# A conv and state-space network on one core: layer 0's parameters turned as one tile, and the first images loaded earlier

## The chip, the cores and the metric

The kernel runs on one core of a Trainium2 chip. The metric is the device time of one execution in microseconds (us), as the median of several runs. Five engines work side by side, each with its own instruction queue: PE (TensorE, matrix products; PEld is its loading of weights), DVE (VectorE), ACT (ScalarE), POOL (GpSimd) and SP (SyncE, which here does nothing but issue transfers). An engine takes its instructions in the order in which they stand in its queue; an instruction that must wait for another engine or a transfer holds up all that stands behind it.

## What is computed

Layer 0 is an inverted-residual block on 32 images of 96 channels and 56 x 56 pixels, layer 1 a block of two selective state-space (Mamba) steps over the 3136 pixels of each image. What matters here is layer 0:

```python
h = conv1x1(x, fake_quant(w1))            # 96 -> 576 channels
h = silu(bn(h, g1, b1, m1, v1))
h = depthwise3x3(h, fake_quant(w2))       # each channel by itself, 9 taps
h = silu(bn(h, g2, b2, m2, v2))
s = silu(mean(h) @ se_w1.T + se_b1)       # 24 values per image
s = sigmoid(s @ se_w2.T + se_b2)          # a gate per channel
h = conv1x1(h * s, fake_quant(w3))        # 576 -> 96
x = x + bn(h, g3, b3, m3, v3)
...
x = layer1(x)
```

`fake_quant` rounds a weight tensor to 255 steps of its largest absolute value; `bn` is a scale `inv` and a shift `sh` per channel.

## The kernel before

Layer 0 keeps the 576 hidden channels in five tiles of up to 128 partitions (`NCT` = 5; the last, `FOLD`, has 64 channels and holds the upper half of the image on 64 partitions and the lower half on the other 64). For each image, `expand` (line 212) makes a hidden tile with matmuls of `w1` and writes it with ACT (line 225) into one of three padded buffers `hpad`. The nine taps of a tile are then done in one of two ways: tiles 2 and 3 with nine passes of DVE (`taps_dve`, lines 300 and 302; `FOLD` likewise, 314 and 316), tiles 0 and 1 (`PE_TILES`) with 32 x 32 matmuls on PE (`taps_pe`, line 276), with ACT's silu behind them (line 283). The silu needs the scale and shift of the second normalisation per partition.

On PE the taps write each group of 32 channels to a place that depends on the band of rows: in band `r` of four, group `gr` goes to group `(gr + r) % 4`. So what stands on a partition in band `r` is another channel than in band 0, and every per-channel parameter used afterwards is needed in four turned copies. `SEEN` lists the eleven versions (two tiles in four bands, and the three others as they are); `NSEE` = 11. The turned parameters are the scale `tinv`, the shift `tsh`, the gate's bias `tseb`, the last convolution's weights `tw3` (96 columns) and the first gate weights `tsew1` (24 columns). They are made by `turned` (line 149), which for each of the five copies each version with transfers inside SBUF: one for an unturned tile, two for `FOLD`, four for a turned one. All are issued by SP (line 161), as are the loads of the weights (line 110) and of the images (line 210, `load_x`). `folded` (line 164) does the like for three small parameters of `FOLD`.

The order of the start: the scheduler of the language places the instructions of everything ahead of `tc.manual_schedule()`; inside it, the order is the one written. SP's queue holds the weight loads, then the turning and folding, then the first three images, and then per image four stores of `x1d` and one load. DVE's queue holds two of the three clearings of `hpad` (line 200), the maxima for the quantisation (line 130), the normalisations (lines 85 to 88), 44 small copies (line 184), the third clearing, the quantisation (lines 132 to 138), the diagonal tap weights (line 193), the clearing of `hfold` (line 203), and then the taps of image 0.

Of the kernel before, what the change touches and what calls it, by code (L numbers as in the profile page):

```python
# [11 lines left out]
F32 = mybir.dt.float32  # L12
# [7 lines left out]
B, C, H, W = 32, 96, 56, 56  # L20
L = H * W
HID, RED = 576, 24
NCT = 5
# [17 lines left out]
FOLD = NCT - 1  # L41

SEEN = [(ct, r) for ct in PE_TILES for r in range(4)] + [(ct, 0) for ct in range(NCT) if ct not in PE_TILES]
NSEE = len(SEEN)


G1, B1, M1, V1, G2, B2, M2, V2, SEB2, TAP = 0, 1, 2, 3, 4, 5, 6, 7, 8, 9
# [6 lines left out]
def conv_mamba_kernel(ctx, tc, a, out):  # L54
    nc = tc.nc
    v, s, g, pe, sp = nc.vector, nc.scalar, nc.gpsimd, nc.tensor, nc.sync
# [23 lines left out]
    def bn_fold(pool, gam, bet, mean, var, p, n, name):  # L80

        inv = pool.tile([p, n], F32, name=f"inv{name}", tag=f"inv{name}")
        sh = pool.tile([p, n], F32, name=f"sh{name}", tag=f"sh{name}")
        s.activation(inv, var, AF.Sqrt, bias=epsc[:p])
        v.reciprocal(inv, inv)
        v.tensor_mul(inv, inv, gam)
        v.tensor_mul(sh, mean, inv)
        v.tensor_sub(sh, bet, sh)
        return inv, sh
# [5 lines left out]
    with ExitStack() as ph:  # L95
        wts = ph.enter_context(tc.tile_pool(name="l0w", bufs=1))
        small = ph.enter_context(tc.tile_pool(name="l0s", bufs=2))
        xin = ph.enter_context(tc.tile_pool(name="l0x", bufs=3))
# [9 lines left out]
        def loadw(name, shape):  # L108
            t = wts.tile(list(shape), F32, name=name, tag=name)
            sp.dma_start(t, a[name])  # L110
            return t

        def wtile(name, shape):
            return wts.tile(list(shape), F32, name=name, tag=name)

        hp = loadw("hp", [128, NCT, NHP])
        w1 = loadw("w1", [C, HID])
        w3 = loadw("w3", [128, NCT, C])
        sew1 = loadw("sew1", [128, NCT, RED])
        sew2 = loadw("sew2", [RED, NCT, 128])  # L120
        seb1 = loadw("seb1", [RED, 1])

        def fake_quant(w, p, shape, name):

            mx = small.tile([p, 1], F32, name=f"mx{name}", tag=f"mx{name}", bufs=1)
            sc = small.tile([p, 1], F32, name=f"sc{name}", tag=f"sc{name}", bufs=1)
            rs = small.tile([p, 1], F32, name=f"rs{name}", tag=f"rs{name}", bufs=1)
            q = small.tile([p, *shape], F32, name=f"q{name}", tag=f"q{name}", bufs=1)
            axis = AX.X if len(shape) == 1 else AX.XY
            v.tensor_reduce(mx, w, axis, ALU.max, apply_absolute_value=True)  # L130
            g.partition_all_reduce(sc, mx, p, bass_isa.ReduceOp.max)
            v.tensor_scalar(sc, sc, 1.0 / 127.0, None, ALU.mult)
            v.reciprocal(rs, sc)
            v.tensor_scalar(q, w, rs, None, ALU.mult)
            v.tensor_scalar(q, q, ROUND, ROUND, ALU.add, ALU.subtract)
            v.tensor_scalar(q, q, sc, None, ALU.mult)
            v.tensor_sub(q, q, w)
            v.tensor_add(w, w, q)

        fake_quant(w1, C, [HID], "w1")  # L140
        fake_quant(hp[:, :, TAP : TAP + 9], 128, [NCT, 9], "w2")
        fake_quant(w3, 128, [NCT, C], "w3")
# [2 lines left out]
        inv2, sh2 = bn_fold(wts, hp[:, :, G2], hp[:, :, B2], hp[:, :, M2], hp[:, :, V2], 128, NCT, "2")  # L145
        inv3, sh3 = bn_fold(wts, cp[:, G3 : G3 + 1], cp[:, B3 : B3 + 1], cp[:, M3 : M3 + 1], cp[:, V3 : V3 + 1], C, 1, "3")


        def turned(name, t, shape):
            to = wtile(name, [128, NSEE, *shape])  # L150
            for e, (ct, r) in enumerate(SEEN):
                if ct == FOLD:
                    parts = [(slice(h * 64, h * 64 + 64), slice(0, 64)) for h in range(2)]
                elif r == 0:
                    parts = [(slice(0, 128), slice(0, 128))]
                else:
                    parts = [
                        (slice(q * 32, q * 32 + 32), slice((q - r) % 4 * 32, (q - r) % 4 * 32 + 32)) for q in range(4)
                    ]
                for rows, src in parts:  # L160
                    sp.dma_start(to[rows, e], t[src, ct])
            return to

        def folded(name, t):

# [6 lines left out]
        fsh = folded("fsh", sh1[:, FOLD : FOLD + 1])  # L172
        ftap = folded("ftap", hp[:, FOLD, TAP : TAP + 9])

        tinv = turned("tinv", inv2.unsqueeze(2), [1])
        tsh = turned("tsh", sh2.unsqueeze(2), [1])
        tseb = turned("tseb", hp[:, :, SEB2 : SEB2 + 1], [1])
        tw3 = turned("tw3", w3, [C])
        tsew1 = turned("tsew1", sew1, [RED])
        tsew2 = wtile("tsew2", [RED, NSEE, 128])  # L180
        for e, (ct, r) in enumerate(SEEN):
            for q in range(4):
                src = q % 2 * 32 if ct == FOLD else (q - r) % 4 * 32
# [14 lines left out]
        for i in range(NHB):  # L198
            t = hp3.tile([128, H + 2, W + 2], F32, name=f"hpad{i}", tag=f"hpad{i}")
# [1 line left out]
            hpad.append(t)  # L201
        hfold = hp3.tile([128, H // 2 + 2, W + 2], F32, name="hfold", tag="hfold")
        v.memset(hfold, 0.0)

        xs, maps, h2s, pools, se = {}, {}, {}, {}, {}

        def load_x(b):
            if b < B:
                xs[b] = xin.tile([C, L], F32, name=f"x{b}", tag="x")
                sp.dma_start(xs[b], a["x"][b])  # L210

        def expand(b, ct, qs):
            if not 0 <= b < B:
# [187 lines left out]

        P0, P1 = PE_TILES
        D0, D1 = (ct for ct in range(NCT) if ct not in PE_TILES and ct != FOLD)
        load_x(0)
        load_x(1)
        with tc.manual_schedule():
            expand(0, D0, range(4))
            expand(0, P0, range(4))
            for b in range(B + 1):
# [18 lines left out]
                silu_dve(b, D0, 1)  # L428
                project(b - 1, 1)
                load_x(b + 2)  # L430
                expand(b, P1, range(4))
                taps_dve(b, D1, 0, range(6, 9))
# [15 lines left out]
    with ExitStack() as ph:  # L448
# [65 lines left out]
        for i in range(NL):  # L514
# [8 lines left out]
            for h in range(2):  # L523
                cols = slice(h * C, h * C + C)
                ps = bank(f"cw_{i}_{h}")
                for o in range(KC + 1):
                    to = ps[: C + 1, o * C : o * C + C]
# [17 lines left out]
        for h in range(2):  # L545
            for i in range(NL):
                to = wd[h * 64 + 2 * NS : h * 64 + 2 * NS + RANK, i, :, :]
# [6 lines left out]
        for i in range(NL):  # L554
            for k in range(NB):
                for h in range(2):
                    r = slice(h * 64, h * 64 + 64)
                    v.tensor_scalar(dd[r, i, k, :], eye[r, r], dp[r, i, k, 1:2], None, ALU.mult)

        for k in range(NB):  # L560
            ps = bank(f"wf_{k}")
            for h in range(2):
                r = slice(h * 64, h * 64 + 64)
# [464 lines left out]
```

## Time and profile before

| what | value |
|---|---|
| median of 3 runs | 19243.92 us (19236.5 to 19254.51) |
| the profiled execution: its time | 19246.5 us |
| the profiled execution: its span | 19243.6 us |
| layer 0, with the start | about the first 3300 us |
| DVE busy, share of the span | 18041.5 us, 94% |
| DVE busy in the first 50 us | 24.8 us |
| POOL / PE / ACT busy, share of the span | 81% / 75% / 74% |
| one pass of a tap on DVE (line 302), mean | 1989 ns, 1024 times |
| issue of one turning transfer on SP, median | 589 ns, 150 times |

Times in a profile are counted from the start of the span. In a line of the timeline, the first number is the start, the second the length in us of the whole group, then come the engine ("SPq" is SP's issuing of transfers), the line of the kernel, the operation, what it writes and reads, how often, and in brackets how long the engine had been idle and what ended that. A line of waits names who waited for whom: total us, number of times, and the longest.

### The profile page before, as it was taken

To read this page: it belongs to the slowest core of one execution; us is meant where nothing else is said; L and a number is where in the kernel's file an instruction comes from. 1 tells how busy PE (TensorE), PEld (TensorE's weight loads), DVE (VectorE), ACT (ScalarE), POOL (GpSimd) and SP (SyncE) were. 2 spreads that over 40 slices of the span, in tenths; PEclk is the share of its full clock that TensorE was granted. 3 is DMA by queue.
4 is the path that set the end of the run, shared out by engine and by line. 5 is a ranking of instruction groups with operands and counts; after the bars stand their busy time and mean duration, and the time that the engine had idled before them with its cause. 6 is when DMAs were issued, how large, how long until landed. Compare 5 with 4: busy or idle time off the path is not lost.

```text
span 19243.6 us, 282933 instructions
## 1 busy us (share of the span) xinstructions
PE 14489.7 (75%) x105692; PEld 5827.2 (30%) x105692; DVE 18041.5 (94%) x13684; ACT 14174.9 (74%) x23979; POOL 15509.9 (81%) x6606
## 2 busy tenths in 40 slices
PE   7999999677777777777777777777777777777760
PEld 3544444222222222222222222222222222222220
DVE  7888888699999999999999999999999999999993
ACT  3444444688888888888888888888888888888872
POOL 0000000699999999999999999999999999999991
PEclk9999999787777777877787778777877777778875
DMA  1000000355555555555555555555555555555548
GB/s 27 23 26 27 22 26 22 117 163 164 161 161 164 162 161 162 163 163 164 163 163 161 164 163 161 161 163 163 161 161 163 163 164 162 163 162 164 162 159 246
DMA packets 1049037, 2679.90 MB, mean 139 GB/s; under 512 B 129592, under 2 KB 342928, under 8 KB 1035368
## 3 DMA queue, kind: packets, MB, share of 16 engines
q1 hardware_dynamic: 1047656, 2661.80, 43.9%
q8 instruction: 828, 13.57, 0.3%
q14 instruction: 553, 4.53, 0.1%
HBM read 2211.05 MB, written 449.58 MB: 138 GB/s over the span
## 4 chain that ended last, share of the span: by engine, by line
DVE 35%; issue 24%; ACT 22%; PE 12%; POOL 4%; DMA 2%; SPq 1%; DVEq 0%; POOLq 0%; ACTq 0%
DVE hh L863 18%; DVE hc L871 12%; ACT da L831 5%; ACT L587 4%; ACT L588 3%; PE dw L276 3%; PE c L374 3%; POOL bx L851 2%; ACT cp L839 2%; DVE h L302 2%; DMA lr<-x1d 2%; PE bc L700 1%; PE c L223 1%; ACT dl L587 1%; ACT z L587 1%
## 5 line engine op out<-in xcount | busy, mean ns | idle before, releaser
L851 POOL TENSOR_TENSOR bx<-ub,B 128x1568 f32<-128x1568 f32 x3072 | 10975.8, 3573 | 25.2 <-DMA ub<-ud 15.8
L863 DVE TENSOR_TENSOR_SCAN hh<-da,state,bx 128x784 f32<-128x784 f32 x4608 | 8307.1, 1835 | 50.4 <-ACT da L831 44.8
L831 ACT ACTIVATE da<-deltab,acol 128x784 f32<-128x784 f32 x6144 | 5631.3, 917 | 2158.3 <-DVE hh L863 2124.2
L878 POOL TENSOR_TENSOR hc<-hh,C 128x544 f32<-128x544 f32 x3072 | 4210.3, 1371 | 40.2 <-DVE hh L863 28.8
L675 PE MATMUL xs<-xn,wx 97*64 97x392 f32 x12288 | 2907.0, 610 | 1356.5 <-DVE xn L663 1355.9
L871 DVE TENSOR_TENSOR hc<-hh,cp 128x1024 f32<-128x1024 f32 x3072 | 3667.7, 1194 | 0.1
L903 PE MATMUL y<-hc,rel 128*32 128x392 f32 x24576 | 3016.7, 579 | 367.7 <-DVE hc L871 349.2
L377 POOL TENSOR_TENSOR x<-x,x 96x784 f32<-96x784 f32 x128 | 276.5, 2160 | 3148.6 <-ACT x L376 3110.6
L863 DVE TENSOR_TENSOR_SCAN hh<-da,bx 128x784 f32<-128x784 f32 x1536 | 2679.1, 1774 | 53.4 <-ACT da L831 52.6
L675 PEld LDWEIGHTS xs<-xn,wx 97*64 97x64 f32 x12288 | 1307.8, 165 | 2982.0 <-DVE xn L663 1675.1
L302 DVE SCALAR_TENSOR_TENSOR h<-hpad,hp,h 128x1568 f32<-128x1568 f32 x1024 | 2036.3, 1989 | 34.3
L839 ACT COPY cp<-C 128x512 f32<-128x512 f32 x3072 | 1793.7, 584 | 371.6 <-DVE hc L871 369.2
L700 PE MATMUL bc<-xc,wbc 64*64 64x392 f32 x3072 | 975.5, 798 | 655.9 <-ACT xc L587 655.9
L903 PEld LDWEIGHTS y<-hc,rel 128*32 128x32 f32 x24576 | 579.8, 116 | 2092.5 <-issue 1155.1
L276 PE MATMUL dw<-hpad,diag 32*32 32x392 f32 x36864 | 1101.7, 515 | 38.6 <-issue 38.1
L691 PE MATMUL z<-xn,wz 97*64 97x392 f32 x3072 | 729.4, 555 | 480.4 <-ACT xc L686 462.3
L587 ACT ACT_TABLE_LOAD x768 | 985.3, 1283 | 13.8
L374 PE MATMUL c<-h,w3s 128*96 128x392 f32 (+1 forms) x2560 | 963.6, 521 | 40.3 <-DVE w3s L359 40.3
L588 ACT ACT_TABLE_LOAD x768 | 985.3, 1283 | 11.4
L223 PE MATMUL c<-x,w 96*128 96x392 f32 x2048 | 807.9, 551 | 193.1 <-DMA x<-in_x_dram 112.7
L283 ACT ACTIVATE h<-dw,tsh,tinv 128x392 f32<-128x392 f32 x512 | 340.0, 674 | 728.8 <-PE dw L276 728.8
L773 PE MATMUL o<-z,outw 64*96 64x392 f32 x3072 | 796.4, 652 | 97.4 <-DVE z L914 96.7
(156 smaller groups left out, 15639.9 us busy)
## 6 DMA issues: line engine op xcount, KB each, us to landing
deltab<-deltad SPq DMA_DIRECT2D x1536, 392.0 KB, 5.4
ub<-ud SPq DMA_DIRECT2D x1536, 392.0 KB, 5.8
B<-bcd SPq DMA_DIRECT2D x1024, 392.0 KB, 4.3
C<-bcd SPq DMA_DIRECT2D x1024, 392.0 KB, 4.2
deltad<-dl SPq DMA_DIRECT2D x512, 294.0 KB, 3.6
ud<-us SPq DMA_DIRECT2D x512, 294.0 KB, 3.6
x<-in_x_dram SPq DMA_DIRECT2D x32, 1176.0 KB, 7.4
x1d<-x SPq DMA_DIRECT2D x128, 294.0 KB, 2.6
```

Source lines behind the costliest of these rows:

```text
L276: pe.matmul(ps[r][to : to + 32, :HB], diag[src, n, t, :], hb[src, r0 : r0 + RB, dx : dx + W], start=t == 0, stop=t == 8, skip_group_check= ...
L302: v.scalar_tensor_tensor(acc, src, tap, acc, ALU.mult, ALU.add)
L587: s.activation(t, t, func)
L588: s.preload_act_table_set(MAIN)
L675: pe.matmul(d["xs", k][h * 64 : h * 64 + 64, :HB], wx[:, i, o, k * 64 : k * 64 + 64], xn[:, o + h * HB : o + h * HB + HB], start=o == 0, s ...
L831: s.activation(das[at][:, :LC], d["delta", k][:, p, :], AF.Exp, scale=acol[:, j, i, 2 * k + p : 2 * k + p + 1])
L839: s.copy(cps[at], data[n]["C", j][:, :LP])
L851: g.tensor_mul(bx, data[n]["u", k], beside(data[n]["B", j]))
L863: v.tensor_tensor_scan(hhs[at - p][:, p, :], das.pop(at)[:, :LC], bxs.pop(at), state[i][:, t : t + 1] if c % NQ else 0.0, ALU.mult, ALU.add,)
L871: v.tensor_mul(hcs[at - 1][:, :, :LP], hhs[at - 1][:, :, :LP], beside(cps.pop(at)))
L878: g.tensor_mul(hcs[at - 1][:, :, LP:], hhs[at - 1][:, :, LP:], beside(data[n]["C", j][:, LP:]))
L903: pe.matmul(yps[k][r0 : r0 + DB, :HB], rel, hc[:, p, h * HB : h * HB + HB], start=False, stop=j == SG - 1, skip_group_check=True,)
```

## The change

The five parameters per channel now stand side by side in one tile `per` (128 partitions x 5 tiles x 123 columns: `inv2`, `sh2` and the gate's bias in one column each, `w3` in 96, `sew1` in 24). `w3` and `sew1` are loaded straight into it and quantised there; the three single columns are copied in by DVE. A single tile `turn` then takes each version of all 123 columns together, and a turned version takes two transfers, of `128 - 32 r` and `32 r` partitions, in place of four of 32. `load_x(0)` and `load_x(1)` are moved ahead of the quantisation. The readers take views of `turn`.

```diff
+        NPER = 3 + C + RED
+        per = wtile("per", [128, NCT, NPER])
+        w3, sew1 = per[:, :, 3 : 3 + C], per[:, :, 3 + C :]
         hp = loadw("hp", [128, NCT, NHP])
         w1 = loadw("w1", [C, HID])
-        w3 = loadw("w3", [128, NCT, C])
-        sew1 = loadw("sew1", [128, NCT, RED])
+        sp.dma_start(w3, a["w3"])
+        sp.dma_start(sew1, a["sew1"])
         sew2 = loadw("sew2", [RED, NCT, 128])
         seb1 = loadw("seb1", [RED, 1])
...
+        xs, maps, h2s, pools, se = {}, {}, {}, {}, {}
+
+        def load_x(b):
+            if b < B:
+                xs[b] = xin.tile([C, L], F32, name=f"x{b}", tag="x")
+                sp.dma_start(xs[b], a["x"][b])
+
+        load_x(0)
+        load_x(1)
+
         fake_quant(w1, C, [HID], "w1")
         fake_quant(hp[:, :, TAP : TAP + 9], 128, [NCT, 9], "w2")
         fake_quant(w3, 128, [NCT, C], "w3")
...
-        def turned(name, t, shape):
-            to = wtile(name, [128, NSEE, *shape])
-            for e, (ct, r) in enumerate(SEEN):
-                if ct == FOLD:
-                    parts = [(slice(h * 64, h * 64 + 64), slice(0, 64)) for h in range(2)]
-                elif r == 0:
-                    parts = [(slice(0, 128), slice(0, 128))]
-                else:
-                    parts = [
-                        (slice(q * 32, q * 32 + 32), slice((q - r) % 4 * 32, (q - r) % 4 * 32 + 32)) for q in range(4)
-                    ]
-                for rows, src in parts:
-                    sp.dma_start(to[rows, e], t[src, ct])
-            return to
+        for o, t in enumerate((inv2, sh2, hp[:, :, SEB2])):
+            v.tensor_copy(per[:, :, o], t)
+
+        turn = wtile("turn", [128, NSEE, NPER])
+        for e, (ct, r) in enumerate(SEEN):
+            if ct == FOLD:
+                parts = [(slice(h * 64, h * 64 + 64), slice(0, 64)) for h in range(2)]
+            elif r == 0:
+                parts = [(slice(0, 128), slice(0, 128))]
+            else:
+                parts = [(slice(r * 32, 128), slice(0, 128 - r * 32)), (slice(0, r * 32), slice(128 - r * 32, 128))]
+            for rows, src in parts:
+                sp.dma_start(turn[rows, e], per[src, ct])
+        tinv, tsh, tseb = (turn[:, :, o : o + 1] for o in range(3))
+        tw3, tsew1 = turn[:, :, 3 : 3 + C], turn[:, :, 3 + C :]
...
-        tinv = turned("tinv", inv2.unsqueeze(2), [1])
-        tsh = turned("tsh", sh2.unsqueeze(2), [1])
-        tseb = turned("tseb", hp[:, :, SEB2 : SEB2 + 1], [1])
-        tw3 = turned("tw3", w3, [C])
-        tsew1 = turned("tsew1", sew1, [RED])
...
-        load_x(0)
-        load_x(1)
```

In the changed program, SP's queue holds the weight loads, then images 0 and 1, the folding of `inv1` and `sh1`, image 2, the 18 turning transfers and the folding of the taps. DVE's queue has the three new copies ahead of the 44 of line 184. The orders of ACT, PE and POOL are as before.

More of the change, by code (lines that the diff above doesn't have):

```diff
@@ L203, in conv_mamba_kernel @@
         v.memset(hfold, 0.0)
[L205 to L210, printed above, removed]
         def expand(b, ct, qs):
```

## Prediction

> **What bounds the kernel now.** I read the page first for proportions. VectorE (DVE) is busy 94% of the span, so at first sight anything not on DVE should be worth nothing. But that is a mean over 19 ms, and the change touches only the first 0.1 ms, so I read that stage by itself: the busy time of each engine in stretches from the start of the span (columns after the colon: length, then busy us and count for PE, PEld, DVE, ACT, POOL, then the granted clock of TensorE, DMA share, GB/s).
>
> ```profile
> 0.00:25.00 25.00, 0.00 (x0) 0.00 (x0) 22.22 (x97) 4.64 (x6) 1.75 (x9) 1.00 0.15 31
> 25.00:50.00 25.00, 0.00 (x0) 0.00 (x0) 2.58 (x9) 0.00 (x0) 0.00 (x0) 1.00 0.05 1
> 50.00:75.00 25.00, 0.00 (x0) 0.00 (x0) 0.00 (x0) 0.00 (x0) 0.00 (x0) 1.00 0.07 8
> 75.00:100.00 25.00, 0.00 (x0) 0.00 (x0) 0.00 (x0) 0.00 (x0) 0.00 (x0) 1.00 0.10 18
> ```
>
> From about 28 us to 100 us no compute engine does anything. The waits of the first 200 us say for what:
>
> ```profile
> PE c L223 <- DMA x<-in_x_dram: 112.7, 1, 112.7
> DVE h L300 <- ACT hpad L225: 91.4, 1, 91.4
> ```
>
> The first matmul of image 0 waits for the image. The timeline shows why the image is late: SP's queue is in order, the image stands behind 150 small transfers (line 161), and each occupies the queue for about 0.6 us.
>
> ```profile
> 20.73 0.75 DVE L138 TENSOR_TENSOR w<-w,qw 96x576 f32<-96x576 f32 x1
> ...
> 26.38 1.51 DVE L203 MEMSET hfold<- 128x1740 f32 x1 [0.31 <-issue]
> 32.38 19.33 SPq L161 DMA_DIRECT2D tsh<-sh  x30
> 51.76 14.56 SPq L161 DMA_DIRECT2D tseb<-hp  x23
> 66.42 18.94 SPq L161 DMA_DIRECT2D tw<-w  x30
> 85.41 19.00 SPq L161 DMA_DIRECT2D tsew<-sew  x30
> 104.45 1.52 SPq L210 DMA_DIRECT2D x<-in_x_dram  x3
> 112.68 13.91 PE L223 MATMUL c<-x,w 96*128 96x392 f32 x32 [112.68 <-DMA x<-in_x_dram]
> 119.33 1.04 DVE L300 TENSOR_SCALAR h<-hpad,hp 128x1568 f32<-128x1568 f32 x1 [91.44 <-ACT hpad L225]
> 133.87 0.68 ACT L283 ACTIVATE h<-dw,tsh,tinv 128x392 f32<-128x392 f32 x1 [6.23 <-PE dw L276]
> ```
>
> The reader should see three times here: the quantised `w1` is ready at 20.73 + 0.75 = 21.48 us, DVE's own preparation ends at 26.38 + 1.51 = 27.89, and the first matmul starts at 112.68. The chain of waits, cut to the first 130 us, agrees:
>
> ```profile
> by line: SPq L161 56.2%; DVE h L302 8.6%; DVE hpad L200 6.6%; issue 6.6%; DMA x<-in_x_dram 6.2%; PE c L223 4.3%; DVE tsew L184 2.9%; DVE qw L137 1.0%; DVE mxw L130 1.0%; DVE w L138 0.9%; DVE diag L193 0.9%; DVE h L300 0.8%; ACT hpad L225 0.
> ...
> 104.45 8.10 DMA x<-in_x_dram
> 112.68 5.58 PE c L223 x8
> ```
>
> So SP's issue bounds the opening 112.68 us, and DVE bounds what follows.
>
> **What the Trainium skill says.** "DMA: Bandwidth & Descriptors", Anatomy of one DMA, gives a DMA a fixed cost of about 2 us, most of it completion, and its Rules for kernel authors advise merging small transfers and issuing a load early, ahead of compute. The trace agrees on the fixed cost (1.7 us from issue to landing for 0.1 KB), but adds what decides here: these landings overlap, and what doesn't overlap is the queue's 0.64 us per issue (12.02 us for 19). "SBUF — State Buffer", Who interferes with whom, says that a DMA never contends with a compute engine for SBUF; that is why I let the images land beside the quantisation for nothing. The trace of before has no image landing beside DVE work of that kind. "TensorE: Matmul & The Clock Gate", Part 1, says that an idle TensorE starts at half clock for some 3.4 us, not always the same. The trace agrees: the first 8 matmuls of line 223 take 5.58 us, later 8 take 2.90. TensorE is idle ahead of its first matmul in both kernels, so this start-up cost stays.
>
> **The change part by part.**
>
> (a) Turning. Before: 5 tiles x (2 PE tiles x (1 + 3x4) + 2 + 2) = 5 x 30 = 150 transfers. After: 2 x (1 + 3x2) + 2 + 2 = 18, each of 123 columns. So 132 issues go, more than the title's wording gives. At 0.637 us each (79.06 us for the 124 from 25.39 to 104.45) that is 84 us of SP's queue. This is not yet a gain: what counts is when the image and the turned values come.
>
> (b) Images first. SP now issues x0 and x1 directly after the weights: `seb1` went at 4.51, so x0 goes at about 4.94. In both programs an issue waits for the transfer eight before it; for x0 and x1 these are `gpw` and `fusw`, issued at 1.20 and 1.66 and landed in 1.7 and 2.5 us: no wait. Alone in the queue an image took 112.65 - 104.45 = 8.2 us, so x0 lands at 13.1, or up to 1.4 later for (d). `w1` is ready only at 21.5, so the load is hidden with 7 us to spare, and the quantisation is what is late next. finv and fsh (4 small ones) and then the third image follow x1; images moved at 230 to 241 GB/s (105 to 120 us), so three of 1.2 MB take 15 us and are through at about 22, ahead of the turning.
>
> (c) DVE gets three copies of 128x5 ahead of the quantisation. Three reciprocals of that size take 0.28 us together: +0.25. They stand in front of the 44 copies of line 184, all ahead of `w1`. So `w1` is ready at 21.73. With 0.05 for the hand-over (ACT ended at 119.29, DVE began at 119.33) the first matmul starts at 21.8 in place of 112.68: 90.9 us earlier. DVE's first tap pass came 119.33 - 112.68 = 6.65 after it, so at 28.45; DVE is free at 27.89 + 0.25 = 28.14, which just fits. If DVE were late instead, it would cost what it is late, some tenths.
>
> (d) `w3` and `sew1` now land in strips of a wider tile: 640 pieces each (384 B and 96 B) in place of 128. The stretch from 0 to 24 us has 2713 packets at 15.7% of 16 engines, so 22 ns each; 1024 more are 1.4 us of all engines, 0.7 of it ahead of `w3`. The loads were over by 6.6 us by the DMA rate, and DVE reads `w3` at 8.54: hidden. Lower bound 0; upper bound, if a piece cost 60 ns (assumed, nearly three times the mean), 3.8 us for both loads. That reaches about 10.4, where the 44 copies begin anyway. I take 0.
>
> (e) Turning after the quantisation. All 18 read `per`, so they wait for its last write, the `w3` part, 23.23 + 0.65 + 0.25 = 24.1. 18 x 0.64 = 11.5, so the last is issued by about 36.2 and lands at 38, and `ftap` (2 more) at 39. The first reader is ACT's silu of line 283, which came 133.87 - 112.68 = 21.2 after the first matmul, so at 43.0. Its four bands read the first 7 transfers, landed by 31: no wait, 12 us to spare. One transfer of the 18, the eighth, waits for the third image; at about 29 that has landed. `ftap` was read first at 183.65, now near 93. The waits of ACT, DVE and PE that these transfers release have only image 0's own work queued behind them, and all of it comes after 43.
>
> (f) In the loop, the instructions of each engine stand in the same order. Only the views differ: `tw3` rows of 96 with a step of 123, `tseb` with a step of 123. `w3s` (1.25 us, 32 times, on DVE) reads whole rows as before; I take 0. Upper bound, if it fell to half its speed: 32 x 1.25 = 40 us. Below zero there is nothing: no instruction gets shorter.
>
> Sum on the profiled execution: 19243.6 - 90.9 + about 0.3 for small things in (f) = 19153.0. The whole program hangs on image 0 (no other engine has work that doesn't), so it shifts by that amount. The profiled run took 19246.5, the median shown is 19243.92, 0.3 above the span; I take the shift from the median: 19153.3.
>
> **The rivals.**
>
> 1. Part of the gain goes into a new wait: the turned tile is late because the queue is held, for example by the third image, or `w3s` pays for its rows. For: the 18 transfers all stand behind x2 and behind the last write of `w3`. Against: 12 us of slack in (e). With the 40 us of (f) in full, the gain is 51: 19193. If the images' landing and the turning together slipped 25 us, the gain is about 78: 19166; that lies in my range.
>
> 2. The change doesn't do what it says: the stage is bound by something that this trace hides, such as the maxima over partitions on POOL (line 131; a POOL duration is rough, and DVE picks them up at 17.60, after a memset). If these took until 70 us the gain would be about 40: 19204, the edge of no change. Against: DVE did the quantisation at 17.6 to 23.9 with no wait in front, so they were over by then.
>
> 3. Slower: the wider tiles shift the tiles allocated after them in SBUF, and the tap passes (lines 302 and 316) get slower by where their operands lie. Those are 1024 + 256 passes on the engine that bounds layer 0. The gain of 90.9 us is used up at 71 ns for each, 3.6% of 1989 ns; at 6.5% (129 ns) the kernel takes 19318. For: nothing in the profile excludes an address effect by name. Against: the three `hpad` buffers of 13456 B lie at different offsets, and eight passes over each take the same 15.06 us (the undisturbed ones at 168.67, 268.39 and 366.66).
>
> **How the numbers follow.** A measurement of this kernel tells about 0.2%, 38 us, from no change; the three runs shown span 18 us. Forecast (shift of about 91, small costs): 0.86. Rival 1 with a loss of 10 to 50: 0.08, still faster in nearly all of it. Rival 2: 0.03, half of it within 0.2%. Rival 3: 0.03, with 0.02 slower. Faster by over 0.2%: 0.95; within: 0.03; slower: 0.02. The range is the forecast with the scatter of 18 us below, and above with the same plus some of rival 1: 19134 to 19182.
>
> **What would show it.** The first matmul (line 223 of before) at about 22 us, released by DVE and not by a DMA; the first tap pass at 28 to 29; the first silu of the taps at 43, released by PE; 18 transfers of about 0.64 us each between 24 and 37; no stretch without compute after 28; image period and layer 1 as before. Wrong would be: the first matmul past 25, a wait of ACT's first silu for a DMA, tap passes longer than 1852 ns where POOL is idle, or `w3s` over 1.3 us.

## The result, and the profile after

The changed kernel takes 19160.03 us (median of 5 runs, 19144.16 to 19173.51), the kernel before 19243.92 (19236.5 to 19269.49 in 5). The ratio is 0.9954 with a 95% interval of 0.994 to 0.9969: 83.9 us less, with an interval of about 60 to 115. The second set of runs gave 19161.89 against 19248.74, 86.9 us less, at 0.9954 (0.9941 to 0.9968). The forecast was 19153.3, 90.6 us less, in a range of 19134 to 19182.

The busy time of the engines in the first 100 us of the changed kernel (columns as in the table of before: stretch, length, then PE, PEld, DVE, ACT, POOL with counts, granted clock, DMA share, GB/s):

```profile
0.00:25.00 25.00, 3.03 (x5) 1.77 (x6) 22.22 (x97) 4.65 (x7) 1.75 (x9) 1.00 0.75 175
25.00:50.00 25.00, 24.93 (x533) 13.93 (x541) 24.23 (x25) 10.79 (x16) 0.00 (x0) 1.00 0.13 31
50.00:75.00 25.00, 21.72 (x315) 11.65 (x296) 24.47 (x15) 13.71 (x20) 0.00 (x0) 0.86 0.00 1
75.00:100.00 25.00, 21.54 (x443) 12.20 (x413) 24.57 (x15) 14.21 (x27) 0.00 (x0) 0.90 0.01 3
```

The three rows that held no more than 2.6 us of DVE are full. The last column says where the images went: 175 GB/s in the first 25 us, beside DVE's quantisation, whose count and sum (x97, 22.22 us) are those of before. The last column but two says something that the prediction left out: the clock is at 0.86 and 0.90 in rows in which PE works. The timeline of the changed kernel, with the lines that answer to those of before:

```profile
5.51 0.82 SPq L150 DMA_DIRECT2D x<-in_x_dram  x2
...
21.16 0.75 DVE L143 TENSOR_TENSOR w<-w,qw 96x576 f32<-96x576 f32 x1
...
21.97 13.26 PE L226 MATMUL c<-x,w 96*128 96x392 f32 x32 [21.97 <-DVE w L143]
...
24.33 11.35 SPq L175 DMA_DIRECT2D turn<-per  x18
...
26.80 1.51 DVE L213 MEMSET hfold<- 128x1740 f32 x1 [0.30 <-issue]
...
28.27 1.04 DVE L303 TENSOR_SCALAR h<-hpad,hp 128x1568 f32<-128x1568 f32 x1
...
42.36 0.68 ACT L286 ACTIVATE h<-dw,turn 128x392 f32<-128x392 f32 x1 [6.08 <-PE dw L279]
```

The bracket of the first matmul now names DVE and the quantised `w1`, at 21.97 in place of 112.68: 90.7 us earlier. The first tap pass has no bracket: DVE comes to it straight from the clearing of `hfold`, 91.1 us earlier. The first silu of the taps is released by PE and not by a transfer; the 18 transfers are issued by 35.7. (Of the two tensors loaded straight into `per`, only `w3` is quantised there; `sew1` stays as it is loaded. It is `w3` that the turning waits for.)

So 91 us were gained at the start, and 72 arrived in this profiled execution (spans 19243.6 and 19171.7), 84 and 87 in the medians. The start of `w3s`, the gated weights that DVE makes once per image, shows where the lead was lost; it is the same instruction in both programs:

```
image      before    changed   lead, us
1          224.19    134.11    90.1
4          533.43    448.00    85.4
9         1049.59    963.93    85.7
16        1762.87   1690.61    72.3
24        2592.31   2527.11    65.2
32        3398.43   3333.41    65.0
end       19243.6   19171.7    71.9
```

Of 91 us, 26 went within layer 0, in pieces, and 7 came back later. Three questions were open: which of the two edits brought the 91 us; whether the changed kernel is slower in layer 0 by itself; and what bounds the start now.

### The profile page after: what moved, and what is told of

Same layout as the page of the kernel before. It is cut to its first block, busy times and chain, and to the rows that moved or that the text cites. A ratio compares the mean times of both kernels' runs of the same rounds, so it can differ in the third digit from the quotient of the medians.

```text
span 19171.7 us, 282785 instructions
## 1 busy us (share of the span) xinstructions
PE 14498.6 (76%) x105692; PEld 5824.8 (30%) x105692; DVE 18039.9 (94%) x13687; ACT 14175.4 (74%) x23979; POOL 15511.8 (81%) x6606
## 4 chain that ended last, share of the span: by engine, by line
DVE 37%; issue 32%; ACT 20%; PE 5%; POOL 3%; DMA 2%; SPq 1%; DVEq 0%; POOLq 0%; ACTq 0%
DVE hh L864 20%; DVE hc L872 12%; ACT da L832 5%; ACT L588 3%; ACT L589 3%; DVE h L305 2%; ACT cp L840 2%; DMA lr<-x1d 2%; PE bc L701 1%; POOL bx L852 1%; ACT z L588 1%; ACT dl L588 1%; ACT xc L588 1%; POOL x L380 1%; PE xs L676 1%
## 5 line engine op out<-in xcount | busy, mean ns | idle before, releaser
L879 POOL TENSOR_TENSOR hc<-hh,C 128x544 f32<-128x544 f32 x3072 | 4309.9, 1403 | 34.0 <-DVE hh L864 24.9
L286 ACT ACTIVATE h<-dw,turn 128x392 f32<-128x392 f32 x512 | 340.0, 673 | 752.4 <-PE dw L279 752.4
```

What stands on the lines that cost most here:

```text
L879: g.tensor_mul(hcs[at - 1][:, :, LP:], hhs[at - 1][:, :, LP:], beside(data[n]["C", j][:, LP:]))
```

## The experiments

**The same two kernels once more.**

> The kernel before, unchanged, for a second profile. Theory A (the whole gain comes at the start; what layer 0 then gives or takes is chance, set by where the stretches of half TensorE clock fall in an image): the first matmul again at 112.7 us, but the 32nd w3s not at 3398 us again: a difference of 5 to 30 us, with the sum of half-clock time in layer 0 differing the same way. Theory B (the changed kernel is slower by some 25 us in layer 0, always, and the kernel before steady): the 32nd w3s within 3 us of 3398.

> The changed kernel, unchanged, for a second profile and five more times. Theory A: first matmul at 22.0, the 32nd w3s somewhere between 3305 and 3340 us (3333 in the first profile), image period equal to 90 us of busy DVE plus its idle time, and a median 75 to 100 us under the kernel before. Theory B: the 32nd w3s again at 3333 within 3 us, and a median 60 to 75 us under the kernel before.

First matmul at 112.35 and 22.01 us. But the 32nd `w3s` came at 3414.45 in the kernel before, 16 us later than in its first profile, and at 3316.22 in the changed one, 17 us earlier than in its first; the lead at that place lies between 65 and 98 us, by which executions are paired. In this second pair the lead grew within layer 0, from 91.2 us at image 1 to 98.2 at image 32, and 13 us of it went later (spans 19244.5 and 19159.2). A constant loss in the changed kernel (theory B) would have repeated; it didn't.

The period from one `w3s` to the next, compared with DVE's idle time in it (gaps over 0.05 us) and with the time in it in which TensorE's clock was at half (summed from the trace's record of the granted clock), over the first 30 periods of each execution:

```
                  period   DVE idle  half clock  period against idle,   against half clock,
                  us mean  us mean   us mean     slope, correlation     slope, correlation
before            103.1    13.3      10.6        0.94  0.99             0.30  0.81
before, again     103.6    13.8      11.3        0.99  1.00             0.32  0.75
changed           103.9    14.1      12.7        1.01  1.00             0.32  0.82
changed, again    103.3    13.5      11.4        0.97  0.99             0.31  0.74
```

DVE works about 90 us on an image, nearly the same each time, and what it stands idle comes on top, one for one. In the first pair the changed kernel had 12.7 - 10.6 = 2.1 us more of half clock per image; by the slope of 0.31 and over 30 periods that is 20 of the 25 us lost in them. But the second pair doesn't follow this: with 0.1 us more of half clock per image the lead grew by 7 us. So the correlation within an execution explains one pair and not the other. The next two kernels test whether a late PE is behind it.

**PE taken out of the way.** In both kernels:

```diff
-            for t in range(9):
+            for t in (0, 4, 8):
                 dy, dx = divmod(t, 3)
                 for r in range(4):
```

> The kernel before with three of the nine taps in the two tiles that PE does (the other six are left out), so that PE has some 26 us less per image and does not come last. Theory A (DVE's idle time in layer 0 is PE being late, more so when its clock is halved): DVE's idle time per image falls from 13 to under 5 us, the image period to 92 to 95 us, and it no longer follows the half-clock time. Rival (DVE's idle time has another cause): period stays at 103.

> The changed kernel with the same six taps left out in the PE tiles, to be read against the kernel before with them left out. Theory A (layer 0's give and take is only where TensorE's half-clock stretches fall): with PE out of the way the lead of 91 us at the first matmul stays within 3 us through all 32 images. Theory B (the changed kernel is slower in layer 0 by itself, by its views or its queue): the lead shrinks by 10 us or more by the last image.

The period fell to 95.4 and 95.2 us and DVE's idle time to 5.4 and 5.3, both just outside what theory A had named. The waits of DVE at the gate in the kernel before, over 100 to 3200 us, with nine taps and then with three (who waited for whom: total us, times, longest):

```profile
DVE gate L352 <- PE se L350: 343.8, 29, 13.8
```

```profile
DVE gate L352 <- PE se L350: 148.3, 32, 5.7
```

Half clock rose to 27.3 us per image, and the period no longer grows with it (correlation -0.4 and -0.5): with less work for PE, more half clock didn't mean a longer period. And the lead at `w3s` held: 92.5 us at image 1, 90.0 at the lowest, 93.3 at image 24, 96.6 at image 32. It wandered by 4.2 us at most from where it began, a little over the 3 that theory A allowed, and it didn't shrink by the 10 or more of theory B. So in this pair, one execution of each, the changed kernel isn't slower in layer 0 by itself; the give and take with nine taps comes through DVE's waits, most of them at the gate for PE. That the half clock is what makes PE late isn't shown: it rests on the correlation, no run here holds the clock fixed, and the stretches of half clock come behind waits of PE (last section).

**Each edit by itself.** Only the loads of the first images moved, in the kernel before:

```diff
...
+        load_x(0)
+        load_x(1)
+
         fake_quant(w1, C, [HID], "w1")
...
-        load_x(0)
-        load_x(1)
         with tc.manual_schedule():
```

> Only the loads of images 0 and 1 are moved, the 150 turning transfers stay. Theory C (what ended the idle start is the image's place in the queue alone, since turned values are needed only later, each in its turn): SP still issues the turning until about 115 us, the first matmul at 21.6 to 22, first silu of the taps at 42 to 45, small waits of some us for turned values, and a median within 10 us of the changed kernel's. Theory D (both parts are needed, since the silus, the gate and w3s of image 0 then wait for the turning): first matmul at 22 as well, but image 0's w3s at 150 or later in place of 134, and a median 20 to 60 us above the changed kernel's.

First matmul at 21.54. SP's queue and the waits of the first 160 us:

```profile
4.87 0.82 SPq L145 DMA_DIRECT2D x<-in_x_dram  x2
...
37.90 20.93 SPq L171 DMA_DIRECT2D tsh<-sh  x30
...
101.22 20.91 SPq L171 DMA_DIRECT2D tsew<-sew  x30
```

```profile
ACT h L286 <- DMA tsh<-sh: 5.5, 3, 3.4
PE se L343 <- DMA tsew<-sew: 3.7, 4, 1.9
```

The 150 transfers run until 122 us, but beside image 0: only a few of their values come late, 5.5 us for the shifts and 3.7 for the gate's weights. Image 0's `w3s` comes at 145.0, 11 us after that of the changed kernel. The median is 19171.14 against 19248.74, 77.6 us less (ratio 0.9959, 0.9946 to 0.9971). Theory C allowed 10 us between the medians, and they differ by 9.3, with overlapping intervals: the place in the queue is worth most of the gain. The late values cost 11 us of one image, less than theory D said.

Only the one tile, with the loads of the images where they stood:

```diff
-        load_x(0)
-        load_x(1)
-
         fake_quant(w1, C, [HID], "w1")
...
+        load_x(0)
+        load_x(1)
         with tc.manual_schedule():
```

> Only the one tile with its 18 transfers; load_x(0) and load_x(1) stand in the program after everything, as in the kernel before. SP's queue as compiled has image 0 directly after the weights all the same, and images 1 and 2 ahead of the turning, because all 18 transfers wait for the quantised w3. Theory C2 (the place in the program text does nothing here): first matmul at 22, first silu at 42 to 43, a median within 10 us of the changed kernel's. Theory D2 (the early place matters): first matmul at 45 us (18 x 0.64 + 8.2 later than the quantisation), a median 20 us or more above the changed kernel's.

SP's queue in this kernel:

```profile
5.50 0.35 SPq L150 DMA_DIRECT2D x<-in_x_dram  x1
...
12.09 1.05 SPq L150 DMA_DIRECT2D x<-in_x_dram  x2
24.36 11.37 SPq L172 DMA_DIRECT2D turn<-per  x18
```

The scheduler puts image 0 directly behind the weights although it stands last in the text; all 18 transfers wait for the quantised `w3`. First matmul at 22.00, median 19160.99 (ratio 0.9952, 0.9939 to 0.9964): the changed kernel's time. The moved loads add nothing to the one tile. Why the kernel before has all 150 transfers ahead of the image is not shown: those of `tseb`, `tinv` and `tsh` were ready early, but the 30 of `tw`, which wait for `w3` too, stood ahead of it as well.

**The image held back on purpose.** The loads stand last in the text, as in the kernel with only the one tile, and the first two wait for the turned tile:

```diff
             if b < B:
                 xs[b] = xin.tile([C, L], F32, name=f"x{b}", tag="x")
+                if b < 2:
+                    g.tensor_copy(xs[b][:, 0:1], turn[:C, NSEE - 1, 0:1])
                 sp.dma_start(xs[b], a["x"][b])
```

> The one tile with its 18 transfers, and images 0 and 1 held back until the turning is done: POOL writes one column of their tiles from the last of the turned tile, and the loads, which overwrite it, wait for that. SP's queue as compiled then holds the 18 transfers, image 2, image 0, image 1. Theory A (the first matmul's time sets the whole shift): turning done at about 36, its last landing at 38, image 0 behind 5 us of image 2's data, first matmul at 46 to 49 in place of 22; median 24 to 27 us above the changed kernel's, that is 58 to 68 under the kernel before. A rival (the transfers' number counts by itself, not the image's place): within 10 us of the changed kernel.

```profile
48.63 12.76 PE L225 MATMUL c<-x,w 96*128 96x392 f32 x32 [48.63 <-DMA x<-in_x_dram]
```

The line of the timeline names the image again. 112.68 - 48.63 = 64.1 us of lead at the first matmul, and the median is 19188.49 against 19252.27: 63.8 us less (ratio 0.9965, 0.9952 to 0.9977, so 44 to 92 us). With 18 transfers but a late image, only what the image gains is gained.

**What bounds the start now.** First the clearings of `hpad` and `hfold` on POOL:

```diff
-            v.memset(t, 0.0)
+            g.memset(t, 0.0)
             hpad.append(t)
...
-        v.memset(hfold, 0.0)
+        g.memset(hfold, 0.0)
```

> The changed kernel with the four clearings (three hpad, hfold) on POOL in place of DVE: DVE loses 3 x 2.86 + 1.51 us and four gaps of 0.3 to 0.65 in its start. Theory E (after the change DVE's own preparation bounds the start): w1 quantised at 16 to 18, first matmul at 16 to 18 in place of 22, first tap pass at 23 to 24 in place of 28.3, median 3 to 6 us lower, which five rounds can hardly tell. Rival (the maxima over partitions on POOL end only shortly before 17.6, hidden so far behind a clearing, and now stand behind one): DVE waits for POOL at line 137 until 15 to 18, first matmul at 20 to 22, nothing gained.

Neither was right. First matmul at 23.15, later than without the edit; DVE doesn't wait at line 137, but one of its small copies is stretched. The group of the copies (minimum, median and maximum in ns) and POOL's last clearing:

```profile
L194 DVE COPY tsew<-sew x44: 161/163/7415, 7.8 to 11.6; 24x32 f32<-24x32 f32 x44
```

```profile
17.03 1.61 POOL L213 MEMSET hfold<- 128x1740 f32 x1
```

One copy takes 7415 ns, from 11.26 to 18.67, and the group (from 7.77, 10.98 us long) ends at 18.75; POOL's last three clearings run from 11.35 to 17.03 + 1.61 = 18.64. The Trainium skill, "SBUF — State Buffer", Who interferes with whom, says that a DVE copy can take the pair of ports that it shares with GpSimd, and that whoever is second then blocks fully, for the whole instruction of the first. The timing fits a blocked copy, but in two points not that sentence: the copy was held through three clearings in a row, and its start is put 0.09 us ahead of theirs. That the ports are the cause is not shown. Median 19161.47, as the changed kernel.

Then part of DVE's work on ACT, which is idle then (the clearing of the third `hpad`, and the 44 copies as 18 strips):

```diff
-                v.tensor_copy(tsew2[:, e, q * 32 : q * 32 + 32], sew2[:, ct, src : src + 32])
...
+            for to, src in parts:
+                s.copy(tsew2[:, e, to], sew2[:, ct, src])
...
+            if i < 2:
+                v.memset(t, 0.0)
+            else:
+                s.activation(t.rearrange("p y w -> p (y w)"), epsc.to_broadcast([128, (H + 2) * (W + 2)]), AF.Copy, scale=0.0)
```

> The changed kernel with part of DVE's start done by the idle ACT: the third hpad cleared by ACT, and the 44 small copies of line 194 made as 18 by ACT. POOL, whose clearings held one of DVE's copies for 7.4 us in the run before, gets nothing. Theory E (DVE's preparation bounds the start after the change): w1 quantised and first matmul at 16 to 18 in place of 22, first tap pass at 22 to 24 in place of 28.3; the median 4 to 6 us lower, less than five rounds tell. Rival (the maxima on POOL or the image's landing end last): first matmul still at 20 or later, with DVE idle at line 137.

```profile
16.56 13.99 PE L234 MATMUL c<-x,w 96*128 96x392 f32 x32 [16.56 <-DVE w L143]
```

First matmul 5.4 us and first tap pass (23.23) 5.0 us earlier: DVE's own preparation was the bound. Now DVE waits 2.15 us for ACT's `hpad` ahead of that pass. The median, 19149.33 (ratio 0.9949, 0.9935 to 0.9963), can't be told from the changed kernel's.

**The idle time in the loop.** DVE's waits in the changed kernel over layer 0:

```profile
DVE gate L355 <- PE se L353: 373.1, 31, 13.7
DVE hsum L335 <- ACT h L326: 31.6, 12, 5.0
DVE xsum L387 <- POOL x L380: 29.1, 31, 1.0
```

The gate stands in DVE's queue ahead of passes that need nothing from it. They were exchanged:

```diff
+                taps_dve(b, D0, 0, range(5, 9))
                 excite2(b - 1)
-                taps_dve(b, D0, 0, range(5, 9))
                 expand(b, D1, range(4))
-                gated_w3(b - 1)
                 silu_dve(b, D0, 0)
-                taps_dve(b, D0, 1, range(7))
+                taps_dve(b, D0, 1, range(2))
+                gated_w3(b - 1)
+                taps_dve(b, D0, 1, range(2, 7))
```

> The changed kernel with one thing moved in the loop of layer 0: DVE's last four passes of the first half go ahead of the gate's addition, and two passes of the second half between it and w3s, so that DVE has work while PE, late at half clock, finishes taps and gate. Theory A (the idle time that sets the image period is DVE standing in order before the gate for a late PE): DVE's wait at the gate falls from 378 us in all to under 200, the image period from 103 to 97 to 100 us, median 90 to 190 us under the changed kernel's. Rival (PE, busy 93% of the image, is the bound and the wait only moves to a later place): the wait at the gate falls, another of DVE's waits for ACT or PE grows by the same, median within 30 us of the changed kernel's.

```profile
DVE xsum L387 <- POOL x L380: 199.0, 45, 6.3
DVE gate L355 <- PE se L353: 140.3, 31, 6.0
DVE hsum L335 <- ACT h L326: 28.8, 12, 5.8
```

Median 19074.45 against 19253.12: ratio 0.9907 (0.9894 to 0.9921), an interval apart from the changed kernel's, and 87 us below its second median, a little short of theory A's 90. The wait at the gate lost 233 us and the one at `xsum`, for an output that comes from PE through ACT and POOL, took up 170 of them: a part of both theories. The period is 101.0 us, over the 97 to 100 expected.

> Both moves of the two kernels beside it. Theory A and E add: first matmul at 16 to 18 and image period as in the kernel with the gate later; median 0 to 12 us below that kernel's.

Both moves together: first matmul at 16.55, median 19088.4 (0.9915, 0.9901 to 0.9928), not below the kernel with the gate alone, within the scatter of both.

Last, the sums of the first half's output moved behind four more passes:

```diff
-                sum_x(b - 1, 0)
-                taps_dve(b, D1, 0, range(6))
+                taps_dve(b, D1, 0, range(4))
+                sum_x(b - 1, 0)
+                taps_dve(b, D1, 0, range(4, 6))
```

> The kernel with the gate later, and DVE's sums of the first half's output (xsum, which wait for POOL) moved behind four further passes of the second DVE tile. Theory A (each of these waits is DVE standing in order before a late PE, and further work ahead of it fills it): the wait at xsum falls from 199 us in all to under 60, the image period from 101 to 97 to 99, median 40 to 130 us under the kernel with the gate later. Rival (PE is by now the bound): the wait moves on to the next place, median within 30 us of the kernel with the gate later.

```profile
DVE gate L355 <- PE se L353: 172.9, 31, 6.1
DVE hsum L335 <- ACT h L326: 96.5, 25, 6.3
DVE h L303 <- PE c L377: 53.6, 15, 5.0
```

The wait at `xsum` is gone, the three that remain sum to 323 in place of 368 us, and the median is 19076.26 (0.9902, 0.9887 to 0.9917), as before this move. That is what the rival said: a wait taken from one place turns up at the next. PE is busy 2749 of the 2900 us from 200 to 3100, DVE 2550. That PE is the bound by now fits this, but no kernel here takes work from PE with the gate later. Of the kernels that do all nine taps, those with the gate later are the fastest; they beat the changed kernel and the one before.

## Why the prediction was right

- The reading of the first stage by itself, against a DVE that is busy 94% of the span, was right: the idle stretch was worth its length at the first matmul, 90.7 us of the 90.9 forecast.
- But "DVE bounds what follows" holds for the mean over the span and not for layer 0, which comes next. There PE is the busier one in the kernel before (2961 of the 3170 us from 130 to 3300, DVE 2729; columns as above), and DVE waits for it at the gate:

```profile
130.00:3300.00 3170.00, 2960.56 (x42438) 1568.31 (x42422) 2729.16 (x1666) 1400.73 (x2231) 261.44 (x120) 0.95 0.09 24
```

- Step (a), 132 issues fewer, and step (e): 18 transfers from 24.33 to 35.68 (24.1 to 36.2 predicted; its own sum, 24.1 + 11.5, gives 35.6), the first silu at 42.4 (43.0), released by PE. The fixed cost of 2 us that the prediction takes from the Trainium skill, "DMA: Bandwidth & Descriptors", Anatomy of one DMA, stands there for transfers on the GpSimd path. Here SP issues them, and what counts is the measured 1.7 us.
- Step (b): image 0 issued at 5.51 in place of 4.94. The issues of the two loads into strips of `per` take SP 0.65 and 0.63 us in place of 0.43, and the load behind them 0.66 in place of 0.45, which (d) had not priced; the slack of 7 us hid it. The upper bound of (d) was not hidden as it says: DVE reads `w3` at 8.54, so loads over at 10.4 would have held it by up to 1.9 us; they came in time. And (b) gave the loads' new place in the text a part in the gain, and it has none beside the one tile (19160.99 without it). The prediction also didn't say that either edit alone brings most of the gain: the moved loads without the one tile give 77.6 us.
- Step (c): `w1` at 21.91 (21.73), first matmul at 21.97 (21.8), first tap pass at 28.27 (28.45). The 0.2 is the quantisation's read of `w3` in its wider tile, 0.70 us in place of 0.46; (f) priced the strided views in the loop only.
- Step (f): `w3s` 1251 ns in both, the gate's addition 171 in place of 166 ns; the tap passes 1852 ns at the median in both. Rivals 1 to 3 didn't happen.
- The term that was off is in the sum: that the shift of 90.9 us arrives whole at the end. 71.9 and 85.3 arrived in the two profiled pairs, 83.9 and 86.9 in the medians. In layer 0 the period depends on how late PE is, which differs from execution to execution; the prediction had this only as the scatter of 18 us. The intervals of both comparisons hold the 90.6, so no loss beyond chance is shown; that the medians came within 7 us of the forecast is in part luck, since executions of the changed kernel lie 32 us apart.

## What to carry to other kernels

Ask of a start that is bound by a queue what the first matmul waits for, and put that ahead of what is needed later; with a scheduler, look at the compiled order of the queue, since an edit to the text may do nothing, and a dependency may do it unasked. A gain at the start is worth its length only as far as the stages behind it keep their pace; follow one instruction per image through both traces to see, and take what bounds each stage from that stage's own busy times. Where an engine that bounds a loop waits in order for a later engine, move independent work ahead of the wait, until the other engine is the bound.

## What the runs showed of the hardware that was not expected

In layer 0 TensorE's clock fell to half for stretches of 3.4 to 10.2 us, 11 to 13 us per image, and most of them came behind a short wait of PE. An example from the changed kernel, as busy time in windows and with PE's line of the timeline:

```profile
132.50:135.90 3.40, 1.30 (x5) 0.45 (x4) 3.40 (x3) 3.09 (x3) 0.00 (x0) 1.00 0.01 2
135.90:139.30 3.40, 3.40 (x7) 1.55 (x6) 3.33 (x3) 0.29 (x2) 0.00 (x0) 0.50 0.00 0
```

```profile
135.51 5.03 PE L377 MATMUL c<-h,w3s 128*96 128x392 f32 x9 [2.10 <-DVE w3s L362]
```

PE waits 2.1 us for `w3s`, and the clock is at half in the window behind. In each execution the stretches begin on a fixed grid of 3.41 us (to within 0.01). Of the 298 stretches in the four executions of the two kernels, 248 follow a step of the grid in which PE stood idle for over 1 us, 1.7 us at the median; of the 2908 other steps at full clock, 197 have so much. At half clock PE is slower: eight matmuls of line 226 take 5.52 us in the half-clock stretch at 64.11, and 2.90 at full clock at 130.51. So waits of PE and half clock can feed each other, and a correlation between half clock and the period doesn't tell which came first. Why 50 stretches have no such gap ahead of them, and 197 gaps no stretch behind, stays open. With three taps in place of nine, and PE busy 82% in place of 93% of 100 to 3200 us, the clock was at half for 27 us of each image of 95 (mean granted clock 0.85 in place of 0.94 to 0.95).

A DVE copy of 24x32 stood 7.4 us beside three clearings on POOL, which cost more than taking them off DVE had saved.
